# Feed-forward stage of a graph network: comparison lanes, means and weighted rows kept in PSUM, second norm without a ScalarE copy

## The chip, the cores and the metric

The kernel runs on one core of a Trainium2 chip. A core has a matrix engine (PE in the profile), a vector engine (VectorE, DVE), an activation engine (ScalarE, ACT), a general engine (GpSimd, POOL) that here only issues gathers, and a queue for plain transfers (SyncE, SP). They run side by side and wait for each other on semaphores. They work on SBUF, a memory of 128 partitions, and on PSUM, eight banks of 128 x 512 float32 into which PE writes its products. The metric is device time of one execution in microseconds; it is given as the median of several runs.

## What is computed

A graph of 10,000 nodes with 512 features and 160,000 edges, sorted by target, goes through two layers. The first one is a relational layer with a feed-forward part, the second a pair of sage layers:

```python
h = jnp.maximum(_layernorm(x, axis=-1), 0.0)
# layer 0
h_all = jnp.einsum('nd,rdf->nrf', h, rel_W) + rel_b          # four messages of a node
msg = h_all[src, edge_type]
agg = jax.ops.segment_sum(msg, dst, num_segments=n)
agg = agg / jnp.maximum(deg, 1.0)[:, None]                   # mean over a node's edges
x1 = layer_norm(h + h @ self_W + self_b + agg, ln1_w, ln1_b)  # first norm
f = gelu(x1 @ W1 + b1) @ W2 + b2                             # feed-forward
x = x + layer_norm(x1 + f, ln2_w, ln2_b)                     # second norm
# layer 1
h = jnp.maximum(_layernorm(x, axis=-1), 0.0)                 # third norm
# two times: h = relu(h @ W_self + mean of h[src] over dst @ W_neigh + b)
x = x + h
```

W1 is 512 x 1024 and W2 1024 x 512. All is float32.

## The kernel before

**Stages.** There are four of them, one after the other. The first one (up to about 1208 us in the profile) computes the four messages of every node, writes them to a table hall_d in the chip's main memory, and works out index lists from the edges. The second one, the feed-forward stage, which the change touches, gathers messages, takes means, and runs both norms, the feed-forward products and the third norm; it writes h1_d, the rows of the next stage, and xn_d, the new x. The third and fourth stage are the two sage layers, which gather from h1_d and h2_d in the same manner.

**Blocks.** Targets are worked on in blocks of 128 nodes, 79 of them, of which the last one has 16 nodes and is done first. A block's messages come in by gathers: one instruction on POOL (L844) fetches 128 rows of 512 values into a tile `rows` of SBUF, by 128 indices that lie in SBUF. A node's first 11 edges have a gather each (`row`, 11 gathers in a block); what is beyond them is spread over 5 more (`orow`), and a few leftovers are shared among 4 or 16 blocks (`srow`). The tiles come from a ring of 28, so POOL can run ahead until the ring is full.

**Means.** PE adds the rows of `orow` and `srow` into a PSUM tile `pa` (L897), by a product with a one-hot matrix `hot`; VectorE has made it (`hots`, L870) by comparing lane numbers 0 to 127 (`lane`) with the target of each row (`loc`) for seven tiles at a time, 128 x 896 values. The shared rows are split into an upper and a lower half first (L834, L836, L837), and are added in reduced precision. VectorE then adds the 11 `row` tiles into `pa` one by one (`add`, L908). L1176 scales `pa` by the inverse degree and adds the block's own row (`xs`, loaded from xs_d).

**Norms.** `Scales.stats` takes mean and variance of a row block (L1063, L1064) and puts them into columns of a small tile `mv`; `finish` computes scale and shift for all columns at once with a root on ScalarE and two small VectorE instructions (L1070 to L1073); `apply` scales a row block on ScalarE (L1078). In the first norm, apply makes the normed block in place, PE transposes it into `pT` and ScalarE scales the transposed block by ln1_w and ln1_b for the products (`turn`, L1013 and L1015), and VectorE makes `rest`, the same block times ln1_w plus ln1_b and b2, for the residual sum (L1117, L1118). In `second`, VectorE adds the product `po` to `rest` and takes statistics (L1092). In `scaled`, ScalarE applies the second norm to that in place, and VectorE multiplies by ln2_w and adds to the row of x (`xrs`, L1122 and L1123), takes statistics for the third norm, which ScalarE applies one round later into `h1`.

**Order.** The instructions of all engines are written out by one loop over the blocks, and each engine runs its own in that order. In a round for block b: the one-hot matrix of the next block; `second` for products that are done; the additions into `pa`; L1176 and the first norm's statistics; a part of the feed-forward products (`products`, a list of parts made by `Group.parts`: for four blocks two parts with half of the first product each, `up`, and two with the second product of two blocks each, `down`); `finish`; `scaled`; the rest of the part with the transposes of the block before; and `begin`, which issues the gathers of the next block and PE's sums over them. So two rounds in four have a second norm for two blocks.

**PSUM.** The eight banks in this stage: two for `pa` (psA), two for `pT` (psT), two for the first product (psH), two for the second (psO).

Of the kernel before, what the change touches and what calls it, by code (L numbers as in the profile page):

```python
# [8 lines left out]
F32 = mybir.dt.float32  # L9
# [3 lines left out]
AF = mybir.ActivationFunctionType  # L13
OP = mybir.AluOpType
PSUM = bass.MemoryType.PSUM
DRAM = bass.MemoryType.DRAM
P = 128
# [4 lines left out]
def kernel(  # L22
# [33 lines left out]
    nc = tc.nc  # L56
    N, D = x.shape
# [62 lines left out]
    lane = const.tile([P, P], F32, name="lane")  # L120
# [6 lines left out]
    rdeg = const.tile([P, NB], F32, name="rdeg")  # L127
# [14 lines left out]
    def wide(pool, row, n, name):  # L142

        t = pool.tile([P, n], F32, name=name)
        nc.sync.dma_start(t, bass.AP(tensor=row.tensor, offset=row.offset, ap=[[0, P], [1, n]]))
        return t
# [453 lines left out]
    with ExitStack() as s:  # L600
# [4 lines left out]
        psT = s.enter_context(tc.tile_pool(name="psT", bufs=1, space=PSUM))  # L605
# [128 lines left out]
        if N % P:  # L734
            r = sets[0][2]
            residual(rows, r, 0, full)
            for j in sorted(range(R), key=lambda j: (j % RH, j)):
                pm = psM.tile([P, D], F32, name="pm")
                for k in range(KC):
# [7 lines left out]
                                op=OP.subtract)  # L747
# [64 lines left out]
    def aligned(ctxa):  # L812
# [6 lines left out]
        blocks = ([full] if N % P else []) + rest  # L819

        def height(b):
            return min(P, N - b * P)
# [35 lines left out]
                others += tails  # L858
            return others, [rows(P, row[:, b, t:t + 1]) for t in range(own(b))]

        def hots(b, pool, scalar=False):
            n = OT + NL if b < full else OT_LAST
            hot = pool.tile([P, OT + NL, P], F32, name="hot", bufs=2)
            if scalar:
                for t in range(n):
                    nc.scalar.activation(hot[:, t, :], lane, AF.Abs, bias=loc[:, b, t:t + 1],  # L866
                                         scale=-1.0)
                nc.scalar.activation(hot[:, :n], hot[:, :n], AF.Relu, bias=ones[:, :1], scale=-1.0)
                return hot
            nc.vector.tensor_tensor(hot[:, :n].bitcast(F32R),  # L870
                                    lane[:, None, :].to_broadcast([P, n, P]),
                                    loc[:, b, :n].unsqueeze(2).to_broadcast([P, n, P]),
                                    op=OP.is_equal)
            return hot
# [25 lines left out]
        def begin(b, hot, table, pool, idle=None, split=False):  # L900
            others, mine = gather(b, table, pool, split)
            return sums(b, others, hot, idle), mine
# [8 lines left out]
        with ExitStack() as s:  # L911
            ring.append((s.enter_context(tc.tile_pool(name="gat", bufs=1)), RINGS[0]))
            wp = s.enter_context(tc.tile_pool(name="wp2", bufs=1))
            gp = s.enter_context(tc.tile_pool(name="gp", bufs=1))
            sp = s.enter_context(tc.tile_pool(name="sp", bufs=3))
            psT = s.enter_context(tc.tile_pool(name="psT2", bufs=2, space=PSUM))
            psH = s.enter_context(tc.tile_pool(name="psH", bufs=2, space=PSUM))
            psO = s.enter_context(tc.tile_pool(name="psO", bufs=2, space=PSUM))
            w1s = wp.tile([P, KC, F], F32, name="w1s")
# [4 lines left out]
            nodes, xrs = {}, {}  # L924
# [57 lines left out]
            fetch(LATE[0])  # L982
            for b in blocks[:2]:
                load(b)
            first_hot = hots(blocks[0], gp)
            residuals(LATE[0])
            ln1w = wide(wp, ln1_w, D, "ln1w")
            lnb2 = wide(wp, ln1_b, D, "lnb2")
# [8 lines left out]
            ln2w = wide(wp, ln2_w, D, "ln2w")  # L997
# [51 lines left out]
            class Scales:  # L1049
# [27 lines left out]
                def apply(self, out, v, c, r, func):  # L1077
                    nc.scalar.activation(out, v, func, bias=self.rs[:r, 1, c:c + 1],  # L1078
                                         scale=self.rs[:r, 0, c:c + 1])

            rests = {}
            fed, third = [], []
            now = Scales()
# [13 lines left out]
            def scaled(got, first):  # L1097

                nonlocal third, now
                if first:  # L1100
                    b, c = first
                    r, v = height(b), nodes[b]
                    now.apply(v[:r], v[:r], c, r, AF.Identity)
                if third:
                    h1, at = pair(h1_d, third[0][0], len(third), "h1", 2)
                    for k, (b, c) in enumerate(third):
                        now.apply(h1[:, k, :], xrs.pop(b), c, height(b), AF.Relu)
                    nc.sync.dma_start(at, h1)
                third = []
                for b, v, c in got:  # L1110
                    r = height(b)
                    now.apply(v[:r], v[:r], c, r, AF.Identity)
                if first:
                    b, c = first
                    r, v = height(b), nodes[b]
                    rests[b] = gp.tile([P, D], F32, name="rest", bufs=11)
                    nc.vector.tensor_tensor(rests[b][:r], v[:r], ln1w[:r], op=OP.mult)  # L1117
                    nc.vector.tensor_tensor(rests[b][:r], rests[b][:r], lnb2[:r], op=OP.add)  # L1118
                now = Scales()
                for b, v, c in got:  # L1120
                    r = height(b)
                    nc.vector.tensor_tensor(v[:r], v[:r], ln2w[:r], op=OP.mult)  # L1122
                    nc.vector.tensor_tensor(xrs[b], xrs[b], v[:r], op=OP.add)  # L1123
                    third.append((b, now.stats(xrs[b], r)))
                if got:
                    b, n = got[0][0], len(got)
                    nc.sync.dma_start(rows_of(xn_d, (b, n, height(b))), xrs.pop((b, n)))
# [5 lines left out]
            held = begin(blocks[0], first_hot, table, gp, split=True)  # L1133
# [21 lines left out]
            i = 0  # L1155
            grp = None
            for bs in plan:
                for b in bs:
                    r = height(b)
                    if b == bs[0]:  # L1160
                        before, grp = grp, Group(bs)
                    if i + 2 < len(blocks):
                        load(blocks[i + 2])
                    if i + 1 < len(blocks):
                        hot = hots(blocks[i + 1], gp)
                    ready = []
                    if i + 2 < len(LATE):
                        fetch(LATE[i + 2])
                        ready = arrived[-LATE[i + 2]:]
                    if i == 1:  # L1170
                        nc.sync.dma_start(w2s, w2.rearrange("(k p) n -> p k n", p=P))
                    got = second()
                    pa, mine = held
                    add(b, pa, mine)
                    v = nodes[b]
                    nc.vector.scalar_tensor_tensor(v[:r], pa[:r], rdeg[:r, b:b + 1], v[:r],  # L1176
                                                   op0=OP.mult, op1=OP.add)
                    first = (b, now.stats(v[:r], r))
                    part = products(queue.pop(0) if queue else [], turning)
                    next(part)  # L1180
                    now.finish()
                    scaled(got, first)
                    next(part, None)
                    if i + 1 < len(blocks):
                        held = begin(blocks[i + 1], hot, table, gp, split=True)

                    if b == bs[0] and before:
                        queue += before.parts()
                    turning = lambda g=grp, b=b, v=v: g.turn(b, v)
                    i += 1  # L1190
            turning()
            queue += grp.parts()
            while queue or fed or third:
                got = second()
# [10 lines left out]
        for step, (h_d, ws, wn, bs) in enumerate(((h1_d, ws1, wn1, bs1), (h2_d, ws2, wn2, bs2))):  # L1205
            with ExitStack() as s:
                wp = s.enter_context(tc.tile_pool(name="wp3", bufs=1))
                ip = s.enter_context(tc.tile_pool(name="ip", bufs=2))
                psT = s.enter_context(tc.tile_pool(name="psT3", bufs=3, space=PSUM))
# [42 lines left out]
                    load(i)  # L1252
                turn(blocks[0])
                before = None
                held = begin(blocks[0], hots(blocks[0], ip, True), h_d, ip)
                for i, b in enumerate(blocks):
                    r = height(b)
                    load(i + 3)
                    if i + 1 < len(blocks):
                        hot = hots(blocks[i + 1], ip, True)  # L1260
                    pa, mine = held
                    add(b, pa, mine)
                    m = ip.tile([P, D], F32, name="mb")
                    nc.scalar.activation(m[:r], pa[:r], AF.Copy, scale=rdeg[:r, b:b + 1])  # L1264
                    po = psO.tile([P, D], F32, name="po3")
                    hT = hTs.pop(b)
                    for k in range(KC):
                        nc.tensor.matmul(po[:r], hT[:, k, :r], wss[:, k, :], start=(k == 0),  # L1268
                                         stop=False)
                    if before:  # L1270
                        finish(*before)
                    if i + 1 < len(blocks):
                        turn(blocks[i + 1])
                        held = begin(blocks[i + 1], hot, h_d, ip, (wss[:, 0, :], 3))
                    mT = ip.tile([P, KC, P], F32, name="mTb")
                    transposed(psT, mT[:, :, :r], m[:r], r)
                    before = (b, po, mT)
# [319 lines left out]
```

## Time and profile before

| | us |
|---|---|
| median of 3 runs (lowest, highest) | 6226.65 (6225.09, 6230.65) |
| the profiled execution, its time | 6229.31 |
| its span from first to last instruction | 6227.6 |
| first and last gather from hall_d begin | 1208.0, 2902.4 |
| first gather of the third stage begins | 3002.2 |

| between 1265.0 and 2903.3 us | busy us | instructions |
|---|---|---|
| PE | 1560.41 | 3934 |
| DVE | 1221.93 | 2038 |
| ACT | 557.33 | 899 |
| POOL | 1251.32 | 1255 |

The second table is the answer for one stretch of time: 1638.3 us in which the stage runs evenly. "Busy" is the time in which an engine has an instruction of its own in work; the time an engine's sequencer takes to issue the next one is not in it. The vector instructions of this stretch, with the mean time of one and the idle time ahead of it, come from the list of groups for that stretch:

| line | what | count | mean ns | idle before, us |
|---|---|---|---|---|
| L908 | `pa` + `rows`, in PSUM | 854 | 698 | 204.8 |
| L870 | one-hot comparison, 128 x 896 | 77 | 1072 | 0.0 |
| L1176 | `pa` x inverse degree + `xs` | 77 | 751 | 2.7 |
| L1117 | first norm x ln1_w | 77 | 692 | 67.9 |
| L1118 | that + ln1_b + b2 | 77 | 694 | 2.6 |
| L1092 | `po` + `rest` | 73 | 670 | 0.0 |
| L1122 | second norm x ln2_w | 71 | 673 | 11.8 |
| L1123 | that + row of x | 71 | 692 | 2.5 |

On ScalarE, line 1078 applies the norms: 77 times the first (813 ns each), 71 the second (799) and 69 the third (799).

### The profile page before, as it was taken

The page shows a single profiled execution, that of the slowest core. Times are in us where ns is not written, and L with a number is a line of the kernel's source. Part 1 is how long each engine was busy: PE and PEld are TensorE (multiplying, and loading weights), DVE is VectorE, ACT ScalarE, POOL GpSimd, SP SyncE. Part 2 cuts the span into 40 slices and gives each one's busy share as a digit, 9 for nine tenths or more (in the row PEclk, how much of TensorE's full clock was granted, in tenths as well). Part 3 has the DMA queues.
Part 4 walks back from the last instruction along what each step waited for, and adds up shares of the span by engine and source line. Part 5 has one row for each costly group of instructions (what it writes and reads, how often), then busy time and mean ns, then how long its engine had stood idle before and what let it go on. Part 6 is the DMA issues. An engine that isn't in the chain of part 4 may idle for free.

```text
span 6227.6 us, 55230 instructions
## 1 busy us (share of the span) xinstructions
PE 5669.9 (91%) x15103; PEld 2565.6 (41%) x15103; DVE 3657.2 (59%) x7447; ACT 1858.6 (30%) x3672; POOL 3769.6 (61%) x3927
## 2 busy tenths in 40 slices
PE   9999999899999999999788888888879888888888
PEld 4555554444444444444333333333334333333333
DVE  8889999457777777776333434434434444444444
ACT  1026665023333333333322222222222222222221
POOL 0001110167777777774577777777767777777776
PEclk9999999999999999999899999999999999999999
DMA  4333344487888887885677777777778888888877
GB/s 160 118 126 121 127 138 156 144 276 244 255 252 257 247 252 245 255 255 181 203 237 237 234 237 236 236 237 234 237 232 251 251 247 250 251 247 249 251 246 217
DMA packets 503502, 1373.79 MB, mean 221 GB/s; under 512 B 82206, under 2 KB 82206, under 8 KB 503054
## 3 DMA queue, kind: packets, MB, share of 16 engines
q0 software_dynamic: 308768, 1008.91, 54.4%
q1 hardware_dynamic: 193886, 360.20, 15.9%
q8 instruction: 122, 2.00, 0.1%
q14 instruction: 198, 1.62, 0.1%
q10 hardware_dynamic: 528, 1.05, 0.1%
HBM read 1156.54 MB, written 213.30 MB: 220 GB/s over the span
## 4 chain that ended last, share of the span: by engine, by line
DMA 40%; PE 37%; DVE 9%; issue 7%; POOL 5%; ACT 2%; SPq 0%; POOLq 0%; DVEq 0%; ACTq 0%
DMA rows<-h_d,row 20%; PE pm L774 15%; DMA rows<-h_d,orow 13%; PE pa L897 6%; POOL rows L844 5%; DMA rows<-hall_d,row 5%; PE po L1036 4%; DVE pa L908 4%; PE ph L1025 4%; PE pm L678 2%; PE po L1268 1%; PE po L976 1%; DMA rows<-hall_d,orow 1%; DVE st L1063 1%; PE pT L172 1%
## 5 line engine op out<-in xcount | busy, mean ns | idle before, releaser
L908 DVE TENSOR_TENSOR pa<-pa,rows 128x512 f32<-128x512 f32 x2574 | 1799.2, 699 | 2061.9 <-PE pa L897 1212.3
L844 POOL DMA_INDIRECT rows<-h_d,row x1716 | 1622.3, 945 | 522.7 <-issue 285.7
L897 PE MATMUL pa<-rows,hot 128*128 128x512 f32 (+1 forms) x2358 | 1240.4, 639 | 375.9 <-DMA rows<-h_d,orow 321.1
L844 POOL DMA_INDIRECT rows<-hall_d,row x858 | 870.1, 1014 | 268.7 <-issue 111.2
L844 POOL DMA_INDIRECT rows<-h_d,orow x786 | 743.1, 945 | 354.9 <-issue 102.0
L897 PEld LDWEIGHTS pa<-rows,hot 128*128 128x128 f32 (+1 forms) x2358 | 399.7, 192 | 1156.7 <-DMA rows<-h_d,orow 830.1
L844 POOL DMA_INDIRECT rows<-hall_d,orow x393 | 377.4, 960 | 350.5 <-PE pm L678 203.4
L1268 PE MATMUL po<-wss,hTb 128*128 128x512 f32 (+1 forms) x1264 | 588.7, 610 | 0.0
L1036 PE MATMUL po<-w2s,hid 128*128 128x512 f32 (+1 forms) x1264 | 564.4, 600 | 16.7 <-DVE rest L1092 13.5
L1239 PE MATMUL po<-wns,mTb 128*128 128x512 f32 (+1 forms) x1264 | 574.3, 597 | 1.4 <-ACT mTb L173 1.4
L1025 PE MATMUL ph<-x1T,w1s 128*128 128x512 f32 (+2 forms) x1344 | 558.9, 569 | 4.8 <-ACT hid L1027 4.8
L173 ACT COPY mTb<-pT 128x512 f32<-128x512 f32 (+1 forms) x158 | 91.9, 581 | 1231.7 <-PE pT L172 1231.7
L1264 ACT ACTIVATE mb<-pa,rdeg 128x512 f32<-128x512 f32 (+1 forms) x158 | 108.6, 687 | 1131.9 <-DVE pa L908 1128.6
L879 PE MATMUL pa<-wss,ident 128*128 128x512 f32 x936 | 427.5, 593 | 0.0
L513 POOL DMA_INDIRECT win<-rec_d,at x79 | 81.4, 1031 | 528.4 <-PE pe L538 348.0
L1239 PEld LDWEIGHTS po<-wns,mTb 128*128 128x128 f32 (+1 forms) x1264 | 240.5, 191 | 308.5 <-issue 272.8
L1025 PEld LDWEIGHTS ph<-x1T,w1s 128*128 128x128 f32 x1344 | 249.7, 192 | 282.0 <-issue 272.9
L1036 PEld LDWEIGHTS po<-w2s,hid 128*128 128x128 f32 (+1 forms) x1264 | 237.0, 191 | 306.3 <-issue 281.8
L897 PE MATMUL pa<-tail,hot 128*128 128x512 f32 x624 | 307.8, 610 | 48.9 <-DMA tail<-h_d,srow 48.7
L866 ACT ACTIVATE hot<-lane,loc 128x128 f32<-128x128 f32 x1098 | 337.7, 390 | 0.0
L1268 PEld LDWEIGHTS po<-wss,hTb 128*128 128x128 f32 (+1 forms) x1264 | 237.2, 198 | 241.4 <-issue 241.0
L774 PE MATMUL pm<-wrel,hT 128*128 128x512 f32 x624 | 296.5, 597 | 0.0
(304 smaller groups left out, 6344.3 us busy)
## 6 DMA issues: line engine op xcount, KB each, us to landing
hall_d<-p SPq DMA_DIRECT2D x156, 256.0 KB, 2.5
hall_d<-u SPq DMA_DIRECT2D x156, 256.0 KB, 2.5
hb<-h_d SPq DMA_DIRECT2D x156, 256.0 KB, 4.2
rows<-h_d,row POOLq DMA_INDIRECT x1716, 3.8
xg<-in_x_dram SPq DMA_DIRECT2D x39, 512.0 KB, 3.8
xr_d<-xg SPq DMA_DIRECT2D x39, 512.0 KB, 2.8
xs<-xs_d SPq DMA_DIRECT2D x39, 512.0 KB, 6.6
h_d<-h SPq DMA_DIRECT2D x39, 512.0 KB, 4.6
```

The lines of the kernel that those rows point to most:

```text
L678: nc.tensor.matmul(pm, a[:, k, :], w[:, k, :], start=(k == 0), stop=(k == KH - 1))
L774: nc.tensor.matmul(pm, a[:, k, :], w[:, k, :], start=(k == 0), stop=(k == KH - 1))
L844: nc.gpsimd.indirect_dma_start(out=t[:n], out_offset=None, in_=table, in_offset=bass.IndirectOffsetOnAxis(ap=idx, axis=0))
L866: nc.scalar.activation(hot[:, t, :], lane, AF.Abs, bias=loc[:, b, t:t + 1], scale=-1.0)
L879: nc.tensor.matmul(p, ident, w, start=True, stop=True)
L897: nc.tensor.matmul(pa[:r], h, v, start=(i == 0), stop=(i == len(work) - 1))
L908: nc.vector.tensor_tensor(pa[:r], pa[:r], t[:r], op=OP.add)
L1025: nc.tensor.matmul(ph[:, :n], w1s[:, k, f * P:(f + 1) * P], self.xT[:, k, :n], start=(k == 0), stop=(k == KC - 1))
L1036: nc.tensor.matmul(po[:r], self.hid[:, f, c * r:(c + 1) * r], w2s[:, f, :], start=(f == 0), stop=(f == FC - 1))
L1239: nc.tensor.matmul(po[:r], mT[:, k, :r], wns[:, k, :], start=False, stop=(k == KC - 1))
L1264: nc.scalar.activation(m[:r], pa[:r], AF.Copy, scale=rdeg[:r, b:b + 1])
L1268: nc.tensor.matmul(po[:r], hT[:, k, :r], wss[:, k, :], start=(k == 0), stop=False)
```

## The change

Lane numbers are copied once into a PSUM tile `lanes`, in a pool psC of one bank, and the comparison of this stage reads them there. The bank comes from the transposes, which have one buffer in place of two. (In the sage layers `hots` runs on ScalarE as before.) The scaled mean plus the block's own row stays in `pa`: L1176 writes there, the statistics read it there, `apply` reads it there and writes the normed block to `nodes[b]`, and the residual `rest` is made from it by a new method `affine`. `affine` does (v - mean) x w, in place, and then that x scale + another tile, with two instructions on VectorE. The second norm uses `affine` as well, with the row of x as the last operand and target, so that `apply` for it is gone; it now stands ahead of the first norm's residual on VectorE.

```diff
-        def hots(b, pool, scalar=False):
+        def hots(b, pool, lanes=None):
...
-            if scalar:
+            if lanes is None:
...
             nc.vector.tensor_tensor(hot[:, :n].bitcast(F32R),
-                                    lane[:, None, :].to_broadcast([P, n, P]),
+                                    lanes[:, None, :].to_broadcast([P, n, P]),
                                     loc[:, b, :n].unsqueeze(2).to_broadcast([P, n, P]),
                                     op=OP.is_equal)
...
-            psT = s.enter_context(tc.tile_pool(name="psT2", bufs=2, space=PSUM))
+            psT = s.enter_context(tc.tile_pool(name="psT2", bufs=1, space=PSUM))
+            psC = s.enter_context(tc.tile_pool(name="psC", bufs=1, space=PSUM))
...
-            first_hot = hots(blocks[0], gp)
+            lanes = psC.tile([P, D], F32, name="lanes")[:, :P]
+            nc.scalar.copy(lanes, lane)
+            first_hot = hots(blocks[0], gp, lanes)
...
+                def affine(self, out, v, c, r, w, to):
+
+                    nc.vector.scalar_tensor_tensor(v, v, self.mv[:r, c, 0:1], w[:r],
+                                                   op0=OP.subtract, op1=OP.mult)
+                    nc.vector.scalar_tensor_tensor(out, v, self.rs[:r, 0, c:c + 1], to,
+                                                   op0=OP.mult, op1=OP.add)
...
                 if first:
-                    b, c = first
-                    r, v = height(b), nodes[b]
-                    now.apply(v[:r], v[:r], c, r, AF.Identity)
+                    b, c, pa = first
+                    r = height(b)
+                    now.apply(nodes[b][:r], pa[:r], c, r, AF.Identity)
...
                 third = []
+                last, now = now, Scales()
                 for b, v, c in got:
                     r = height(b)
-                    now.apply(v[:r], v[:r], c, r, AF.Identity)
+                    last.affine(xrs[b], v[:r], c, r, ln2w, xrs[b])
+                    third.append((b, now.stats(xrs[b], r)))
                 if first:
-                    b, c = first
-                    r, v = height(b), nodes[b]
+                    b, c, pa = first
+                    r = height(b)
                     rests[b] = gp.tile([P, D], F32, name="rest", bufs=11)
-                    nc.vector.tensor_tensor(rests[b][:r], v[:r], ln1w[:r], op=OP.mult)
-                    nc.vector.tensor_tensor(rests[b][:r], rests[b][:r], lnb2[:r], op=OP.add)
-                now = Scales()
-                for b, v, c in got:
-                    r = height(b)
-                    nc.vector.tensor_tensor(v[:r], v[:r], ln2w[:r], op=OP.mult)
-                    nc.vector.tensor_tensor(xrs[b], xrs[b], v[:r], op=OP.add)
-                    third.append((b, now.stats(xrs[b], r)))
+                    last.affine(rests[b][:r], pa[:r], c, r, ln1w, lnb2[:r])
...
-                        hot = hots(blocks[i + 1], gp)
+                        hot = hots(blocks[i + 1], gp, lanes)
...
-                    nc.vector.scalar_tensor_tensor(v[:r], pa[:r], rdeg[:r, b:b + 1], v[:r],
+                    nc.vector.scalar_tensor_tensor(pa[:r], pa[:r], rdeg[:r, b:b + 1], v[:r],
                                                    op0=OP.mult, op1=OP.add)
-                    first = (b, now.stats(v[:r], r))
+                    first = (b, now.stats(pa[:r], r), pa)
```

More of the change, by code (lines that the diff above doesn't have):

```diff
@@ L1254, in aligned @@
                 before = None
-                held = begin(blocks[0], hots(blocks[0], ip, True), h_d, ip)
+                held = begin(blocks[0], hots(blocks[0], ip), h_d, ip)
                 for i, b in enumerate(blocks):
@@ L1259, in aligned @@
                     if i + 1 < len(blocks):
-                        hot = hots(blocks[i + 1], ip, True)
+                        hot = hots(blocks[i + 1], ip)
                     pa, mine = held
```

## The prediction

> **What bounds the kernel now.** I read the page first: busy shares by slice (part 2), then the costliest groups (part 5). The change is in the feed-forward stage, which gathers from hall_d; by the timeline those gathers run from 1208 to 2903 us. In those slices PE stands at 9 and DVE and POOL at 7, which names PE; but a high busy share is no proof of the pace. So I asked for the waits of POOL and PE inside 1600 to 2900 us, and for line 844, the gather, in the stage and in the two later gather stages.
>
> ```profile
> PE   9999999899999999999788888888879888888888
> DVE  8889999457777777776333434434434444444444
> POOL 0001110167777777774577777777767777777776
> ```
> ```profile
> POOL rows L844 <- issue: 115.1, 378, 0.3
> POOL rows L844 <- DMA rows<-hall_d,row: 57.9, 190, 0.3
> POOL rows L844 <- DMA rows<-hall_d,orow: 36.9, 121, 0.3
> POOL rows L844 <- DVE pa L908: 31.4, 103, 0.3
> ```
> The columns are total wait, times, longest. The longest is 0.3 us for every releaser, the same 0.3 us that lies ahead of every gather: POOL never waits for anybody there. It issues one gather, is 0.3 us in its sequencer, and issues the next. Its 77% busy is a full queue.
>
> ```profile
> L844 POOL DMA_INDIRECT rows<-hall_d,row x847: 942/946/1832, 1271.6 to 2902.4; - x170
> L844 POOL DMA_INDIRECT rows<-hall_d,orow x385: 942/946/1766, 1265.2 to 2887.9; - x193
> ```
> ```profile
> L844 POOL DMA_INDIRECT rows<-h_d,row x1608: 942/946/962, 3099.7 to 6099.2; - x179
> L844 POOL DMA_INDIRECT rows<-h_d,orow x733: 942/946/963, 3109.7 to 6093.0; - x184
> ```
> Minimum, median and maximum in ns: in the feed-forward stage gathers stretch to 1.83 us, in the later stages none passes 963 ns. What stretches them stands in the timeline (start, duration, both in us):
>
> ```profile
> 2046.63 0.69 DVE L1123 TENSOR_TENSOR xr<-xr,rest 128x512 f32<-128x512 f32 x1
> 2046.77 1.36 POOL L844 DMA_INDIRECT rows<-hall_d,row  x1 [0.30 <-DMA rows<-hall_d,row]
> 2047.35 0.69 DVE L1063 BATCH_NORM_STATS2 st<-xr 128x6 f32<-128x512 f32 x1
> 2048.08 0.18 DVE L1064 BATCH_NORM_AGGREGATE mv<-st 128x2 f32<-128x6 f32 x1
> 2048.18 1.06 DVE L870 TENSOR_TENSOR hot<-lane,loc 128x896 fp32r<-128x896 f32 x1
> 2048.44 1.62 POOL L844 DMA_INDIRECT rows<-hall_d,row  x1 [0.30 <-issue]
> 2049.16 0.69 DVE L1092 TENSOR_TENSOR rest<-po,rest 128x512 f32<-128x512 f32 x1
> ```
> Both long gathers start inside a VectorE instruction with two SBUF inputs, and both end 0.8 us after it. I went through the timeline for all 1,255 gathers after 1265 us. 897 overlap no such instruction and take 942 to 962 ns, whatever one-input statistics or PSUM-and-SBUF sums (L908, L1092, L1176) run beside them; 358 overlap one and take 1127 ns on average, 200 of them over 990. That is the pace of the stage.
>
> [...] here the 128x512 sum with PSUM (L908) takes 698 ns against 692 from SBUF (L1117), so I charge 6 ns. [...] here 813 ns (L1078 from SBUF) against 687 (L1264, the same shape from PSUM, in the sage layers).
>
> **The change part by part.** Everything against the profiled execution: span 6227.6 us, time 6229.3, which is 2.7 above the median 6226.65. POOL's account from 1265.2 to 2903.3 us is 1638.1 us. 1,255 gathers at 0.945 + 0.300 make 1562.5. Busy 1251.3 less 1255 x 0.945 = 1186.0 leaves 65.3 of stretch. About 10 us are waits for free row tiles before 1361 us. I shared each stretched gather's excess among the overlapping two-input instructions by their overlap: the one-hot comparison L870 31.5 us (0.40 each), first norm L1117 and L1118 10.8, second norm L1122 and L1123 20.6 (0.29 a pair), splitting L834 and L836 2.1.
>
> 1. Lane numbers in PSUM. The comparison keeps one SBUF input (loc). In L908 the PSUM operand stands first and the SBUF one second, the same form, and no gather stretches beside it. -31.5 us on POOL. VectorE +6 ns each, 78 times: beside POOL, nothing. The added ScalarE copy of 128x128 into PSUM comes once; 128x128 takes 388 ns on L866, and ScalarE is idle for 69.7 us up to 1245.4, so it is over before the comparison at 1209.8: nothing.
> 2. First norm in PSUM. L1176 writes pa in place, the statistics and ScalarE read it there, and two scalar_tensor_tensor with one SBUF input each (ln1w, lnb2) replace L1117 and L1118. -10.8 us on POOL. Each takes 751 ns (L1176, the same form) for 693: +0.12 us of VectorE a block, and the ScalarE step is 0.12 us shorter.
> 3. Second norm. Two scalar_tensor_tensor replace ScalarE's copy and two VectorE instructions. Both inputs are still in SBUF, so they still stretch gathers. No row shows this form; bounds: no stretch at all (-20.6 us) to a hold twice as long (+20.6). I take 0.75 against 0.69 us; a gather is caught if it starts inside, and then waits for the rest, so the cost goes with the square: 20.6 x 1.18 = 24.3, +3.7 us. 79 ScalarE activations of 0.80 us go; ScalarE is busy 557 of 1638 us there, so in the stage that is worth nothing on the path. VectorE no longer waits for it (11.8 us in all), and where a second norm is in hand the wait of L1117 for ScalarE (67.9 in 77) falls behind other work. VectorE isn't the bound, so neither is counted.
> 4. One transpose buffer in place of two. A block's transposes now need the four ScalarE copies of the block before to be done. I compared each block's first transpose with the end of the preceding copies: the copies end 7.7 us earlier at the closest. Nothing; were ScalarE 7.7 us later, PE would stall.
> 5. pa is held longer: from the end of L1176 to the end of the first norm's second product, which now stands behind the second norm's work (two pairs and two statistics, some 4.8 us). The next use of that buffer, two blocks on, starts 14.8 us or more after L1118 ends today. So 10 us remain. Nothing.
> 6. Order: the second norm comes ahead of the first in VectorE's queue, so the store of xn_d is issued about 1.5 us earlier on SP's queue and the residual's last product later, which nothing waits for until ten blocks on (11 buffers). Nothing.
>
> Sum on POOL: -31.5 - 10.8 + 3.7 = -38.6. Before 1361 us POOL is held by full row tiles (waits of 1.0, 1.5, 1.4, 2.2 us), and faster gathers only wait longer: +1.5, an estimate from 2.5 us of stretch there. After the last gather the chain of waits runs through ScalarE's copies of the second norm at 2911.6 (1.4), 2962.8 (1.4) and 2990.7 (0.8): -3.6, less 0.2 for longer products. Total -40.5.
>
> Does POOL still set the pace? PE does its bare work in 19.4 us a block (sums start at 1419.21, 1438.99 and 1457.96, without a wait), 77.5 for four; four blocks now take 84.2 (2103.90 to 2188.06), and with 65.25 gathers at 1.245 and 1.3 us of stretch they would take 82.5. PE's waits for ScalarE's upper halves and for L1092 (11.6 and 13.5 us in 1300) add 1.5 in four blocks. PE has 3.5 us left in 82.5. What is late next is PE, close behind. Forecast: 6226.65 - 40.5 = 6186.
>
> **Rivals.** (a) PE takes over: if it can't run its four blocks under 83.8 (its granted clock was 0.97 to 0.98 in this stage[...]), 0.4 of 84.2 us is won in each of 15 rounds that POOL sets, and the earlier ones keep theirs: some 16 us with the tail, 6210. For it: PE busy 95%. Against: from 1380 to 1600 us it ran 19.4 a block at a high clock. (b) The change doesn't do what it says: the stretch goes with the length of an instruction or its broadcast operand, not with where its inputs lie. Then only the tail is won: 6223. Against: 897 unstretched gathers. (c) The second norm's pairs catch no gather either: 20.6 + 3.7 more, 6162. (d) Slower: VectorE becomes the bound. It is busy 1221.9 us in 77 blocks, 15.9 each, and waits 2.2 for ScalarE's roots and copies: 18.1 of POOL's 21.2. If PSUM in place as source and target cost a second pass (four products +0.75, comparison +1.07, so +4.1), it would need 22.2, and the stage would grow by 1.0 x 77: 6304. It decides from +3.1 us a block. Against: L1176 with its three operands takes 751 ns, L908 in place in PSUM 698.
>
> **How the numbers follow.** Main case 0.80, 6186, with 6174 to 6198 of its own; (a) 0.08; (b) 0.05; (c) 0.03; (d) 0.04. The range 6170 to 6207 takes in the doubtful size of the second norm and most of (a). A measurement of this kernel tells about 0.2% (12 us) from no change. Faster by more: main, (a), (c), 0.91; within: (b), 0.05; slower: (d), 0.04.
>
> **What would show it.** Gathers from hall_d at a mean near 965 ns instead of 997 (1251.3 / 1255), still 1.245 apart; none stretched beside the comparison or the first norm's products, some beside the second norm's; the last of them at about 2866 instead of 2903 us; ScalarE's groups at line 1078 from four to three. The forecast is wrong if gathers wait for row tiles after 1400 us, or if the comparison from PSUM takes over 1.2 us.

## The result

| | us, median (lowest, highest) | runs |
|---|---|---|
| before | 6229.32 (6225.09, 6232.53) | 6 |
| changed | 6178.40 (6174.73, 6180.58) | 6 |

The ratio is 0.9919, with a 95% interval of 0.9906 to 0.9931: 50.9 us less. The forecast was 6186, 40.5 less than its 6226.65. The profiled execution of the changed kernel took 6174.73 us with a span of 6172.9; it is the quickest of its six, so its span is 54.7 below that of before.

**The gathers.** First the same answer as before for line 844, the gathers of the feed-forward stage (minimum, median and maximum in ns):

```profile
L844 POOL DMA_INDIRECT rows<-hall_d,row x847: 941/946/1472, 1270.8 to 2853.8; - x170
L844 POOL DMA_INDIRECT rows<-hall_d,orow x385: 942/946/1407, 1264.4 to 2839.8; - x193
```

The longest gather has gone from 1.83 to 1.47 us, and the last one starts at 2853.8 us instead of 2902.4. From the list of groups for 1265 to 2904 us (count, busy us, mean ns, idle before), the commoner kind in the kernel before and then in the changed one:

```profile
L844 POOL DMA_INDIRECT rows<-hall_d,row x847 | 859.7, 1015 | 261.0 <-issue 108.8 <-DMA rows<-hall_d,row 44.8 <-DMA rows<-hall_d,orow 27.7
```
```profile
L844 POOL DMA_INDIRECT rows<-hall_d,row x847 | 817.8, 966 | 261.7 <-issue 92.9 <-DMA rows<-hall_d,row 52.4 <-DMA rows<-hall_d,orow 23.5
```

The mean falls by 49 ns and the idle time ahead doesn't move: POOL still issues without a pause, with shorter instructions. Where a gather is still stretched shows in the timeline of the changed kernel (start, duration; L1086 and L1088 are the two products of `affine`):

```profile
2036.29 0.95 POOL L844 DMA_INDIRECT rows<-hall_d,row  x1 [0.30 <-DVE rs L1075]
2036.40 0.74 DVE L1086 SCALAR_TENSOR_TENSOR rest<-rest,mv,ln2w 128x512 f32<-128x512 f32 x1
...
2037.18 0.75 DVE L1088 SCALAR_TENSOR_TENSOR wself<-rest,rs,wself 128x512 f32<-128x512 f32 x1
2037.54 1.22 POOL L844 DMA_INDIRECT rows<-hall_d,row  x1 [0.30 <-issue]
...
2041.16 0.73 DVE L1086 SCALAR_TENSOR_TENSOR pa<-pa,mv,ln1w 128x512 f32<-128x512 f32 x1
2041.88 0.94 POOL L844 DMA_INDIRECT rows<-hall_d,row  x1 [0.30 <-DVE pa L1086]
2041.92 0.75 DVE L1088 SCALAR_TENSOR_TENSOR rest<-pa,rs,lnb 128x512 f32<-128x512 f32 x1
2042.59 1.08 DVE L870 TENSOR_TENSOR hot<-lanes,loc 128x896 fp32r<-128x896 f32 x1
2043.13 0.95 POOL L844 DMA_INDIRECT rows<-hall_d,row  x1 [0.30 <-issue]
```

The gather at 2037.54 starts inside a product of the second norm, both inputs in SBUF, and ends 0.83 us after that product. The one at 2036.29 started 0.11 us ahead of such a product and runs its usual 0.95. The one at 2043.13 starts in the middle of the comparison, now with its lane numbers in PSUM, and isn't stretched: before, a gather that the comparison held up lost 0.43 us on average.

**Where the time went**, for the two profiled executions, from the timelines:

| us | before | changed | difference |
|---|---|---|---|
| first gather of the even stretch begins | 1265.2 | 1264.4 | -0.8 |
| stretch of the gathers over 0.945 us, summed | 65.3 | 18.7 | -46.6 |
| waits for row tiles after that, beyond the usual 0.30 us | 4.8 | 3.7 | -1.1 |
| last gather from hall_d ends | 2903.3 | 2854.7 | -48.6 |
| from there to the first gather of the third stage | 98.9 | 94.7 | -4.2 |
| from there to the end | 3225.4 | 3223.6 | -1.8 |

The line from the changed kernel's timeline that carries the fifth row; the idle time of POOL stands in brackets (98.90 in the kernel before):

```profile
2949.35 0.94 POOL L844 DMA_INDIRECT rows<-h_d,orow  x1 [94.65 <-DMA h_d<-h]
```

### The profile page after: what moved, and what is told of

Same layout as the page of the kernel before. It is cut to its first block, busy times and chain, and to the rows that moved or that the text cites. A ratio compares the mean times of both kernels' runs of the same rounds, so it can differ in the third digit from the quotient of the medians.

```text
span 6172.9 us, 55148 instructions
## 1 busy us (share of the span) xinstructions
PE 5643.4 (91%) x15103; PEld 2563.5 (42%) x15103; DVE 3671.8 (59%) x7447; ACT 1799.6 (29%) x3594; POOL 3722.7 (60%) x3927
## 3 DMA queue, kind: packets, MB, share of 16 engines
q0 software_dynamic: 308768, 1008.91, 54.7%
## 4 chain that ended last, share of the span: by engine, by line
PE 40%; DMA 39%; DVE 8%; issue 6%; POOL 5%; ACT 1%; SPq 0%; POOLq 0%; DVEq 0%; ACTq 0%
DMA rows<-h_d,row 21%; PE pm L774 15%; DMA rows<-h_d,orow 13%; PE pa L897 6%; PE ph L1028 6%; POOL rows L844 5%; PE po L1039 5%; DMA rows<-hall_d,row 3%; DVE pa L908 3%; PE pm L678 2%; PE po L1273 1%; PE po L977 1%; PE pT L172 1%; DVE st L1066 1%; PE po L1244 1%
## 5 line engine op out<-in xcount | busy, mean ns | idle before, releaser
L844 POOL DMA_INDIRECT rows<-hall_d,row x858 | 828.2, 965 | 269.8 <-issue 95.0
```

What stands on the lines that cost most here:

```text
L844: nc.gpsimd.indirect_dma_start(out=t[:n], out_offset=None, in_=table, in_offset=bass.IndirectOffsetOnAxis(ap=idx, axis=0))
```

## The experiments

To compare them, every gather of 985 ns or more was put down to the VectorE instruction with two SBUF inputs that ended 0.82 us before the gather's end (the gather is "caught by" it). Ahead of the runs stood two theories: a gather is caught by an instruction with two SBUF inputs (the prediction), or by a long one or one with a broadcast operand. And one open term: the second norm's pairs cost 17 us of stretch in the changed kernel, where 24.3 were forecast.

**One part alone, and one part undone.** The first four ran on one chip, on which the kernel before took 6225.0 (6217.3 to 6230.98).

e1_lanes:

```diff
-                                    lane[:, None, :].to_broadcast([P, n, P]),
+                                    lanes[:, None, :].to_broadcast([P, n, P]),
...
+            lanes = psC.tile([P, D], F32, name="lanes")[:, :P]
+            nc.scalar.copy(lanes, lane)
```

> Only the lane numbers go to PSUM (with one transpose buffer); both norms stay as before. If the stretch comes from two SBUF inputs: no gather is caught by the comparison any more, stretch of the gathers from hall_d 65.3 - 31.5 = 34 us, time 31 us less, 6198. If it comes from the length of an instruction or its broadcast operand, which stay as they were: stretch 65, time 6229.

e2_first, with `affine` for the first norm alone:

```diff
-                    now.apply(v[:r], v[:r], c, r, AF.Identity)
+                    now.apply(nodes[b][:r], pa[:r], c, r, AF.Identity)
...
-                    nc.vector.tensor_tensor(rests[b][:r], v[:r], ln1w[:r], op=OP.mult)
-                    nc.vector.tensor_tensor(rests[b][:r], rests[b][:r], lnb2[:r], op=OP.add)
+                    now.affine(rests[b][:r], pa[:r], c, r, ln1w, lnb2[:r])
...
-                    nc.vector.scalar_tensor_tensor(v[:r], pa[:r], rdeg[:r, b:b + 1], v[:r],
+                    nc.vector.scalar_tensor_tensor(pa[:r], pa[:r], rdeg[:r, b:b + 1], v[:r],
```

> Only the mean and the first norm stay in PSUM, in the order of before. Two SBUF inputs: stretch 65.3 - 10.8 = 54.5 us, time 10 less, 6219. Length: the products get 60 ns longer, so stretch 67 and time 6230.

e3_second, with `affine` for the second norm alone:

```diff
+                last, now = now, Scales()
...
-                    now.apply(v[:r], v[:r], c, r, AF.Identity)
+                    last.affine(xrs[b], v[:r], c, r, ln2w, xrs[b])
+                    third.append((b, now.stats(xrs[b], r)))
...
-                now = Scales()
...
-                    nc.vector.tensor_tensor(v[:r], v[:r], ln2w[:r], op=OP.mult)
-                    nc.vector.tensor_tensor(xrs[b], xrs[b], v[:r], op=OP.add)
-                    third.append((b, now.stats(xrs[b], r)))
```

> Only the second norm loses ScalarE's copy, in the order of the changed kernel. As the prediction reckoned: the second norm's pairs stretch gathers by 24 us instead of 20.6, the tail is 3.6 us shorter, time 6229. If the three-operand product itself is caught less often: its pairs stretch by 17 us as in the changed kernel, and time is 7 less, 6222.

e4_sbuf_lanes, from the changed kernel:

```diff
-                                    lanes[:, None, :].to_broadcast([P, n, P]),
+                                    lane[:, None, :].to_broadcast([P, n, P]),
```

> The changed kernel with the comparison reading its lane numbers from SBUF again. Two SBUF inputs: the comparison catches gathers for 31.5 us again, stretch 18.7 + 31.5 = 50 us, time 6178 + 31 = 6209. Length or broadcast: no difference, 6178.

| | median us | ratio to before, 95% interval | stretch us | caught by the comparison | by the first norm | by the second |
|---|---|---|---|---|---|---|
| before | 6225.0 | | 65.3 | 70, 29.9 us | 61, 16.5 us | 66, 18.0 us |
| e1_lanes | 6204.06 | 0.9957 to 0.9981 | 37.7 | 0 | 62, 18.6 | 67, 18.2 |
| e2_first | 6219.13 | 0.9984 to 0.9997 | 57.2 | 69, 33.0 | 0 | 64, 22.6 |
| e3_second | 6209.26 | 0.9964 to 0.9984 | 49.7 | 40, 18.6 | 59, 19.8 | 35, 8.8 |
| e4_sbuf_lanes | 6196.29 | 0.9942 to 0.9969 | 39.6 | 68, 25.8 | 0 | 37, 12.0 |
| changed (its own runs) | 6178.40 | 0.9906 to 0.9931 | 18.7 | 0 | 0 | 55, 17.1 |

(The row for before has the stretch of the profile the prediction read.) Where an instruction's first input moves to PSUM it catches nothing, in every run. The comparison alone shows this at equal length, before and in e1_lanes (line 870 in the answer for that line, ns):

```profile
L870 DVE TENSOR_TENSOR hot<-lane,loc x79: 558/1079/1086, 1209.8 to 2872.0; 128x896 fp32r<-128x896 f32 x78, 128x384 fp32r<-128x384 f32 x1
```
```profile
L870 DVE TENSOR_TENSOR hot<-lanes,loc x79: 557/1076/1084, 1207.7 to 2845.9; 128x896 fp32r<-128x896 f32 x78, 128x384 fp32r<-128x384 f32 x1
```

Nearly the same median, same broadcast operands, 70 caught gathers against none. It isn't that no gather came at a bad moment: in e1_lanes 63 of them start well inside a comparison (0.1 us after its start to 0.15 us before its end), and the longest of these took 0.948 us. The rival of length and broadcast falls. In time the part is worth less than in stretch: the median of e1_lanes is 20.9 us below that of the kernel before, where 31 were expected and the stretch fell by 27.6.

What wasn't expected is in the other columns: the parts don't add up. With the lanes back in SBUF (e4_sbuf_lanes) 20.9 us of stretch come back, not 31.5, because the second norm then catches 37 instead of 55. And e3_second, which was to win 3.6 us at best on POOL, takes 15.6 us off: 11.3 at the comparison, which it doesn't touch, and 9.2 at the second norm, while the first norm catches 3.3 more. Its time was 15.7 us below the kernel before, and so below both times that were expected.

**Why the parts depend on each other.** I took all pairs of a gather and a two-SBUF-input instruction after 1400 us, in these kernels and those of the next set (ten in all), and sorted them by the gather's start counted from the instruction's start. Here a gather counts as caught if it ends some 0.82 us after the instruction, however long it took. For sums and products of 128x512 (0.69 us) all 450 gathers that start 50 to 550 ns into it are caught, 2 of 94 that start in its first 50 ns, and none of the 87 in the 0.2 us before it or the 33 that start past 600 ns. For three-operand products (0.75 us) all 236 from 100 to 650 ns are caught, and one in 184 outside. So for one form the two starts decide.

The late end of these windows needs care. A caught gather ends 0.82 us after the instruction, and an undisturbed one takes 0.945, so a start in the instruction's last 0.125 us loses nothing: past 570 ns (620 for the three-operand form) the gathers took 942 to 950 ns, and caught and undisturbed can't be told apart. Time is lost from 50 to 570 and from 100 to 620 ns, 0.52 us for both forms, though one takes 60 ns more.

The next gather starts 0.30 us after a caught one has ended, so 1.12 us after the instruction, when an instruction that follows directly is over or nearly so. It shows in the counts. Of the two-SBUF-input instructions that start within 0.3 us of the end of another one, 445 of 660 catch a gather if the one ahead caught none, and none of 403 if it did (in the ten kernels). This is how e3_second changed the comparison: there 53 comparisons stand directly behind the first norm's last product, against 19 before. Behind the 35 products that had caught a gather no comparison caught one; behind the other 18 every one did. How the second norm's drop in e4_sbuf_lanes comes about isn't shown in this way.

**The second norm.** Three kernels beside the changed kernel itself, on one chip on which the kernel before took 6226.78 (6220.57 to 6232.36).

> The changed kernel itself once more, to stand beside the next three on one chip: 50 us below the kernel before, stretch of the gathers from hall_d 18.7 us, of which the second norm's pairs 17.

e5_order, from the changed kernel (the block of the first norm moved ahead of that of the second):

```diff
-                for b, v, c in got:
-                    r = height(b)
-                    last.affine(xrs[b], v[:r], c, r, ln2w, xrs[b])
-                    third.append((b, now.stats(xrs[b], r)))
                 if first:
                     b, c, pa = first
...
                     last.affine(rests[b][:r], pa[:r], c, r, ln1w, lnb2[:r])
+                for b, v, c in got:
+                    r = height(b)
+                    last.affine(xrs[b], v[:r], c, r, ln2w, xrs[b])
+                    third.append((b, now.stats(xrs[b], r)))
```

> The changed kernel with the first norm's residual ahead of the second norm on VectorE, as before. If the second norm catches fewer gathers than reckoned because of its place in the order: its pairs stretch by 24 us, as reckoned, instead of 17, and time is 7 us more than the changed kernel's. If it is the three-operand product itself: 17 us and no difference.

e7_no_second is the changed kernel without the edit of e3_second.

> Lane numbers and first norm in PSUM, second norm as before with ScalarE's copy. By the prediction's sums: stretch 65.3 - 31.5 - 10.8 = 23 us, the tail 3.6 us longer than the changed kernel's, so 8 us more time than it. If the parts depend on each other by the moments at which gathers start, the stretch is elsewhere, between 10 and 35 us.

e6_staged, from the changed kernel with the order of e5_order:

```diff
-                    last.affine(xrs[b], v[:r], c, r, ln2w, xrs[b])
+                    t = psT.tile([P, KC, P], F32, name="pT").rearrange("p k n -> p (k n)")
+                    last.apply(t[:r], v[:r], c, r, AF.Identity)
+                    nc.vector.tensor_tensor(t[:r], t[:r], ln2w[:r], op=OP.mult)
+                    nc.vector.tensor_tensor(xrs[b], t[:r], xrs[b], op=OP.add)
...
-                    if i == len(work) - 1:
-                        yield
                     if i == len(work) // 2 and turned:
                         turned()
+                    if i == len(work) - 1:
+                        yield
```

> The changed kernel with the second norm applied by ScalarE into the transposes' PSUM bank and finished by two VectorE instructions from there, the transposes moved ahead of the root on ScalarE. If POOL still sets the pace: the stretch falls from 18.7 to under 3 us, the tail grows by 4, time is 12 us less than the changed kernel's. If PE or VectorE takes over: the gathers begin to wait for row tiles after 1400 us, and time is the same or more.

| | median us (lowest, highest) | stretch us | caught by the second norm | last gather ends | from there to the third stage |
|---|---|---|---|---|---|
| again | 6176.80 (6173.31, 6177.05) | 19.2 | 54, 17.1 us | 2857.6 | 94.4 |
| e5_order | 6175.62 (6174.73, 6178.23) | 17.2 | 45, 14.8 | 2854.2 | 96.3 |
| e7_no_second | 6184.92 (6184.31, 6186.48) | 22.5 | 59, 20.5 | 2859.1 | 98.9 |
| e6_staged | 6177.65 (6173.54, 6178.07) | 1.7 | 0 | 2842.3 | 109.3 |

e7_no_second came out as the prediction's sums have it: 22.5 us of stretch for 23 forecast, and 8.1 us more time than the changed kernel. So the second norm's edit is worth 8 us once the other two are in: 3.3 on POOL and 4.5 after the last gather. Its place in the order isn't what makes it cheaper; e5_order gives a little less stretch, not more, and the same time.

e6_staged wins on POOL what it was to win: last gather 15.3 us earlier. It loses 14.9 after it, and its time is that of the changed kernel. The waits of the two kernels from the last gather on (total, times, longest), first e6_staged, then again:

```profile
POOL rows L844 <- DMA h_d<-h: 109.3, 1, 109.3
DVE rs L1075 <- ACT rs L1073: 32.0, 7, 15.5
...
PE pT L1016 <- DVE xr L1131: 8.0, 1, 8.0
```
```profile
POOL rows L844 <- DMA h_d<-h: 94.4, 1, 94.4
DVE rest L1102 <- PE po L1039: 27.9, 5, 7.6
DVE rs L1075 <- ACT rs L1073: 23.2, 7, 8.0
```

With the second norm staged in the transposes' bank, the last block's transposes wait 8.0 us for VectorE to leave it, and ScalarE's copies of the second norm are back among the waits of the last rounds. How much of the 14.9 us each of them costs isn't shown. While gathers ran, PE didn't stop for that bank but once at the start, for 8.2 us before 1420.

**Staging in the loop alone, and a throwaway sum.** e8_staged_loop is e6_staged with the staging only while gathers run (`if first and i + 1 < len(blocks)`, else `affine`). The next two add one sum a block to it, which nothing reads:

```diff
+                    if b < full:
+                        nc.vector.tensor_tensor(spare, lnb2[:, :384], ln1w[:, :384], op=OP.add)
```

`spare` is the unused rest of the lanes' bank in PSUM; in e10_psum_sum `spare` is the first input too, in place of `lnb2`.

> As e6_staged, but the second norm is staged in PSUM only while gathers run; after the last gather it goes the short way of the changed kernel, without ScalarE's copy. If the 15 us that e6_staged won on POOL were lost only after the last gather: last gather at 2842 again, first gather of the next stage 95 us later instead of 109, time 14 below the changed kernel's, 6163. If PE has become the pace: still about 109 us after the last gather, and 6177.

> e8_staged_loop with one throwaway VectorE sum of 128x384 a block, both inputs in SBUF, result in an unused part of PSUM. Two SBUF inputs: 78 sums catch about a third of the gathers that start near them, stretch grows from 2 to 6 to 12 us. VectorE isn't the pace, so nothing else changes.

> The same throwaway sum, its first input in PSUM: same length, stretch stays at 2 us. If length counted, it would grow as in e9_sbuf_sum.

> The kernel of e8_staged_loop once more, since its first run met a chip that granted PE a clock of 0.90. At a clock of 0.98: last gather at 2842, first gather of the next stage 95 us later, 64 us below the kernel before. If PE has become the pace, or the way the second norm is staged costs PE more than the 15 us won on POOL: no more than 50 us below.

These four met chips that granted PE a clock of 0.90, where all the others had 0.98, and on which the kernel before took 7071.82 and 7063.85 us. There e8 took 7117.92 (ratio 1.0045 to 1.0070) and, the second time, 7088.92 (1.0019 to 1.0051), so it was a little slower than the kernel before; e9_sbuf_sum took 7121.86 and e10_psum_sum 7134.79. Beyond the usual 0.30 us, the gathers of e8 waited for row tiles for 361 and 352 us in the stage: POOL isn't the pace there. So neither of its theories was tried under its own conditions, and whether e8 beats the changed kernel at a clock of 0.98 stays open. Nor was the changed kernel run at 0.90.

The throwaway sums don't need the pace, since they are read from single gathers. First e9_sbuf_sum, then e10_psum_sum (the answer for the tile `lanes`, and that for line 844):

```profile
L1180 DVE TENSOR_TENSOR lanes<-lnb,ln1w x77: 566/566/624, 1266.2 to 3165.5; 128x384 f32<-128x384 f32 x77
...
L844 POOL DMA_INDIRECT rows<-hall_d,row x847: 940/946/1292, 1271.6 to 3179.3; - x170
```
```profile
L1180 DVE TENSOR_TENSOR lanes<-lanes,ln1w x75: 566/566/567, 1266.2 to 3163.4; 128x384 f32<-128x384 f32 x75
...
L844 POOL DMA_INDIRECT rows<-hall_d,row x847: 943/949/1149, 1271.3 to 3221.2; - x170
```

Both sums take 566 ns. The one with two SBUF inputs caught 20 gathers for 5.5 us in all, at the low end of the 4 to 10 expected; the one with an input in PSUM caught none, though 13 gathers started well inside it (the longest took 0.949 us). With e1_lanes this settles which property counts: where the inputs lie, not length or broadcast, and not where the result goes either, since both sums write to PSUM. Why a gather waits there, no run shows.

One instruction with a single input catches gathers too: L834, which takes the upper halves of a shared tile in SBUF, 128x512 in 0.42 us where the sums of that size take 0.69. In the ten kernels at a clock of 0.98 all 34 gathers that start 40 to 260 ns into it end 0.82 us after it. One of them, in the changed kernel (start, duration):

```profile
1591.03 0.42 DVE L834 TENSOR_SCALAR rows<-rows 128x512 int32<-128x512 int32 x1
1591.17 1.09 POOL L844 DMA_INDIRECT rows<-hall_d,row  x1 [0.30 <-PE pa L897]
```

So one input in SBUF isn't safe by itself. The tables put none of these catches down to a norm or the comparison; in e6_staged six of them are 0.8 of the 1.7 us that are left.

## Why the prediction was right, and where it was off

1. **POOL sets the pace, stretched gathers are the loss.** Right. The time between the first and the last gather of the even stretch fell by 47.8 us, and 46.6 of that are stretch. A gather takes 960 ns on average, for 965 forecast, and the last one starts at 2853.8 us, for 2866.
2. **Lane numbers in PSUM, -31.5 us.** Right as to what is caught: 70 gathers before, none in e1_lanes. There the stretch falls by 27.6; the comparison's own catches were 29.9 by their release, and the first norm then catches 2 more. The comparison got 8 ns longer on average (1072 to 1080), for 6 forecast. The copy into `lanes` took 0.27 us at 1174.6, hidden.
3. **First norm in PSUM, -10.8 us.** e2_first: 8.1 less stretch alone; nothing is caught by it. By release its share was 16.5 rather than 10.8: sharing an excess by overlap gave some of it to neighbours. Terms 2 and 3 together came out as forecast, 42.8 less stretch in e7_no_second for 42.3; alone they gave 35.7. That the sum fits so closely is in part luck, since the prediction had nothing on how one catch moves the next. The products take 743 and 751 ns on average, as said. ScalarE's step became 35 ns shorter (813 to 778), not 120: the stand-in, L1264 (687 ns), was a different form, with a scale alone where this step adds a shift.
4. **Second norm, +3.7 us on POOL.** This is the term that failed, and with some 7 us the largest part of the 10.4 missed. The prediction let the cost go with the square of the length, so that a longer instruction costs more. The runs show that time is lost over 0.52 us in the longer form as in the shorter one, and how the starts fall decides the rest: 54 catches of 0.32 us instead of 59 of 0.35, -3.3 us instead of +3.7 (again against e7_no_second). What it said of the last rounds held: -3.4 forecast, 98.9 to 94.7 measured.
5. **One transpose buffer, and pa held longer: nothing.** Right. In the waits of PE between 1265 and 2855 us there is none for either (total, times, longest; all five that are listed):

```profile
PE pa L897 <- DMA rows<-hall_d,orow: 20.1, 14, 2.8
PE pa L897 <- ACT upper L837: 14.1, 11, 2.1
PE po L1039 <- DVE rest L1102: 12.3, 15, 1.0
PE po L977 <- DVE rows L979: 6.4, 2, 3.2
PE po L1039 <- DVE rows L979: 3.2, 1, 3.2
```

6. **+1.5 us before 1361.** Not seen: the waits for row tiles after 1265 are 3.7 us, 1.1 less than before.
7. **The rivals.** Rival (a), PE as the pace, didn't come. PE is close behind, as said: it is 96.5% busy (1533.71 of 1590 us), and its waits for `orow` rows fell from 36 to 20 us, but POOL still goes without a pause. The granted clock in the stage was 0.98 before and 0.99 after (1.00 in both from 1380 to 1600 us). Rival (b), length or broadcast, fell with e1_lanes and e10_psum_sum. Rival (c), no catches by the second norm, is refuted by 55 catches. Rival (d), VectorE as the bound through PSUM, has no support: the products of `affine` take 743 and 751 ns in PSUM, and 731 to 754 in SBUF. The line for PE's `orow` waits before, from 1265 to 2903.3 us, to set beside the first one of term 5:

```profile
PE pa L897 <- DMA rows<-hall_d,orow: 36.0, 34, 3.2
```

## What to carry to other kernels

Where POOL issues gathers without a pause, look at the spread of one gather's time, not at its mean: here a minimum of 942 and a maximum of 1832 ns of one instruction form said that something held it up. Then look for VectorE instructions with two SBUF inputs beside the long ones (here they held up 197 of the 200 gathers of 985 ns or more), and for quick ones like L834 (0.42 us). Here moving one input to PSUM took the hold-up away at under 10 ns an instruction (1072 to 1080 for the comparison, 698 against 692 for a sum); the three-operand products cost 40 to 60 ns more than sums, wherever their inputs lay (743 and 751 ns in PSUM, 731 to 754 in SBUF, a sum 692). Don't add up such savings from single parts, and check what a new use of a buffer does after the loop, where e6_staged gave back all it had won.

## What the runs showed of the hardware that was not expected

- Whether a gather is caught by a 128x512 sum in SBUF follows from its start: from about 50 ns after the sum's start it ends 0.82 us after the sum, where an undisturbed one takes 0.945; so it loses time up to 0.125 us before the sum's end.
- A three-operand product of the same size takes 0.75 us instead of 0.69, but its window opens 50 ns later, so time is lost over 0.52 us in both.
- An instruction with two SBUF inputs that starts within 0.3 us of the end of one that caught a gather never caught one itself (0 of 403, against 445 of 660 behind one that had not).
- A one-input instruction in SBUF that does 128x512 in 0.42 us (L834) catches gathers as well (34 of 34).
- At a granted clock of 0.90 instead of 0.98 the kernel before took 13% more time (7064 to 7072 against 6225 to 6229 us), more than the 9% by which 0.98 exceeds 0.90. Where the rest goes wasn't looked into.
